# Layer 0 of a graph network: the node's term added in PSUM, the positive parts on ACT, the sums on DVE

## The chip, the cores and the metric

One core of one Trainium2 chip runs one launch of the whole network. The metric is the device time of that launch in microseconds. Engines: PE is TensorE (PEld its weight loads), DVE is VectorE, ACT is ScalarE, POOL is GpSimd, SP is SyncE. The profile is that of one execution; the time before is the median of three runs.

## The reference, cut to what matters

There are 6250 nodes with 64 features and 206250 edges, sorted by their destination. Layer 0 (the only one that the change touches) forms a message for each edge from the features of its destination and 16 features of the edge, and takes the mean of the positive parts at each node:

```python
h = jnp.maximum(_layernorm(x, axis=-1), 0.0)
msg = jax.nn.relu(jnp.concatenate([h[dst], edge_attr_16], -1) @ W1 + b1)
summed = jax.ops.segment_sum(msg, dst, num_segments=N)
aggr = summed / jnp.maximum(count, 1.0)[:, None]
x = x + jax.nn.relu(aggr + h @ Wres + bres)
```

Write A for the node's part of the product (64 rows of `W1`, and `b1`) and E for the edge's part (16 rows of `W1`). A is the same for all edges of a node, so a message is relu(A + E) = max(E, -A) + A. After layer 0 come another normalisation and three attention layers (`L1_gnn`) over the same edges.

## The kernel before, in words

All is in float32. The prologue of `gnn_kernel` ranks the nodes by their degree, so that 49 tiles of 128 nodes are formed in which node p of a tile is row p, and all nodes of a tile have nearly the same number of edges: tile `b` has room for `CAP[b]` edges per node (66, 46, 44, ... 24, 22) and every node of it has at least `LEAST[b]`. `k.full` holds 1 or 0 for each place between the two, whether the node has that edge. `project(q)` (L344) writes for each node a row of `tabx`: with the weights `wn` (L250 to L252) the row holds -A, then A plus the residual product (`Wres`, `bres`), and x from the input.

`layer0` (L480) goes over the tiles `b` in an order written out by hand for POOL, PE, ACT and DVE (`manual_schedule`, L637); each engine takes its instructions in the order in which the code issues them. Per tile: POOL issues the gathers of the edges' features (`load_e`, four tiles ahead, five buffers), of the node rows `rx` (`load_x`), of the sources (`load_src`) and of the attention layers' edge features (`load_ea`), and scatters finished rows (`put`). `turn(b + 1)` transposes the next tile's edge features on PE, eight edges to a 128x128 transpose, and ACT copies them to `eT` (L529). `messages(b, todo)` (L531) then works in blocks of 16 edges: PE multiplies `eT` by the block-diagonal `w0blk` into a `pm` tile (two buffers of two PSUM banks). `r` names the half of the rows of `eT` (0 to 63 or 64 to 127) that hold four edges, and with it the bank; `u` names the group of eight edges. DVE takes max(E, -A) out of PSUM into `msg` (L546 for a full block, L550 and L556 where places may be empty). A tree of additions on DVE sums `msg` (L568). Where at most three places may be empty (`few`), these columns stay out of the tree and are added one by one with their 1 or 0 (L572); in the two tiles with more, they are multiplied by it first (L562).

Between blocks `messages` takes one piece of work of the group of tiles before (`between`): groups of 8, 8, 8, 8, 8, 4, 3 and 2 tiles (`FIN0`) are finished together. `finish(g)` (L575) divides the sums, adds `rx[..., D:2 * D]`, and for a node without edges (it can only be in the last tile) adds back -A (L587 to L592); the positive part plus x is the new x. DVE then takes its mean (L596, L597), and the pieces are: `squares` on ACT (L602), nothing, `norm` on DVE (L606, L608), and per four tiles `project` (transposes on PE into `pt`, ACT into `ht`) and `rows` (products into `po`, L620, ACT to `k.rows`, L622). When all tiles are done a value is read by all engines, and `attention` runs three times: there every edge's row is fetched by one row gather of POOL (`pick`, L466) into `kv`, with products of the edge features (L809) and DVE work on them; the last layer puts rows in place by products with one-hot matrices (L940).

Of the kernel before, what the change touches and what calls it, by code (L numbers as in the profile page):

```python
# [22 lines left out]
F32 = mybir.dt.float32  # L23
# [4 lines left out]
AF = mybir.ActivationFunctionType  # L28
OP = mybir.AluOpType
# [3 lines left out]
P = 128  # L33
N, E, D = 6250, 206250, 64
# [63 lines left out]
def gnn_kernel(ctx: ExitStack, tc: tile.TileContext, x, src_t, dst_t, dst_row, ea16, ea32, eaT16, eaT32, w, out):  # L98
    nc = tc.nc
# [16 lines left out]
    with tc.manual_schedule(engines={getattr(mybir.EngineType, e) for e in ("Pool", "PE", "Activation", "DVE", "SP")}), \  # L116
# [129 lines left out]
        for l in range(LAYERS):  # L246
            nc.gpsimd.memset(k.wblk[l], 0.0)
            for j in range(4):
                nc.sync.dma_start(k.wblk[l][j * 32:(j + 1) * 32, j * D:(j + 1) * D], w[f"L1_gnn_We{l}"])
        wn = p.tile([D + 1, 2 * D], F32, name="wn")  # L250
        nc.gpsimd.tensor_scalar(wn[:, :D], w0[:, :D], -1.0, 0.0, op0=OP.mult, op1=OP.add)
        nc.gpsimd.tensor_add(wn[:, D:], w0[:, :D], w0[:, D:])  # L252
        sff = p.tile([P, T], F32, name="sff")
        nc.gpsimd.tensor_copy(sff, sf)
        for t, values in ((k.cap, CAP), (least, LEAST)):
# [88 lines left out]
        def project(q):  # L344
            po = psum.tile([P, 4, 2 * D], F32, name="pr_o")
            n = len(quads[q])
            for i in range(n):
                nc.tensor.matmul(po[:, i, :], k.ht[q % 2][:, i * P:(i + 1) * P], wn, start=True, stop=True)
# [131 lines left out]
def layer0(tc, ea16, ea32, ident, tabx, srcs, k, col, least, ones, bad, nbad_i):  # L480

    nc = tc.nc
    with tc.tile_pool(name="g0", bufs=3) as gp, tc.tile_pool(name="e0", bufs=2) as ep, \
# [45 lines left out]
                nc.scalar.copy(eT[:, i0:i1], ps[:, :i1 - i0])  # L529

        def messages(b, between):  # L531
            g, c = group[b], CAP[b]
            nega = st["rx", g][:, b - first[g], :D]
            eT = st.pop(("eT", b))
            msg = ep.tile([P, MAXC, D], F32, name="msg")
            for t0 in range(0, c, 16):
                n = min(16, c - t0)
                pm = pp.tile([P, 2, 2, 4, D], F32, name="pm")
                for u in range(2):
                    for r in range(2):  # L540
                        if u * 8 + r * 4 < n:
                            h = slice(r * D, (r + 1) * D)
                            nc.tensor.matmul(pm[:, r, u].rearrange("p j f -> p (j f)"), eT[h, t0 // 8 + u, :],  # L543
                                             k.w0blk[h, :], start=True, stop=True)
                if t0 + 16 <= LEAST[b]:
                    nc.vector.tensor_tensor(msg[:, t0:t0 + 16], pm.rearrange("p r u j f -> p (r u j) f"),  # L546
                                            nega[:, None, :].to_broadcast([P, 16, D]), op=OP.max)
                elif n == 16:
                    for r in range(2):
                        nc.vector.tensor_tensor(  # L550
                            msg[:, t0:t0 + 16].rearrange("p (u r j) f -> p r u j f", u=2, r=2)[:, r], pm[:, r],
                            nega[:, None, None, :].to_broadcast([P, 2, 4, D]), op=OP.max)
                else:
                    for q in range(-(-n // 4)):
                        m = min(4, n - q * 4)
                        nc.vector.tensor_tensor(msg[:, t0 + q * 4:t0 + q * 4 + m], pm[:, q % 2, q // 2, :m],  # L556
                                                nega[:, None, :].to_broadcast([P, m, D]), op=OP.max)
                if between:
                    between.pop(0)()
            few = range(LEAST[b], c) if c - LEAST[b] <= 3 else ()  # L560
            if c > LEAST[b] and not few:
                nc.vector.tensor_mul(msg[:, LEAST[b]:c], msg[:, LEAST[b]:c],  # L562
                                     k.full[:, WOFF[b]:WOFF[b + 1], None].to_broadcast([P, c - LEAST[b], D]))
            total = st["sum", g][:, b - first[g]:b - first[g] + 1, :]
            c -= len(few)
            while c > 1:
                h = c // 2
                nc.vector.tensor_add(msg[:, :h] if c > 2 else total, msg[:, :h], msg[:, c - h:c])  # L568
                c -= h
            for i, j in enumerate(few):  # L570
                w = WOFF[b] + i
                nc.vector.scalar_tensor_tensor(total, msg[:, j:j + 1], k.full[:, w:w + 1], total,  # L572
                                               op0=OP.mult, op1=OP.add)

        def finish(g):  # L575

            n, b0 = FIN0[g], first[g]
            bs = slice(b0, b0 + n)
            rx, s = st.pop(("rx", g)), st.pop(("sum", g))
            wide = lambda t: t[:, :n, None].to_broadcast([P, n, D])  # L580
            c = wp.tile([P, GN], F32, name="cnt")
            nc.vector.tensor_scalar(c[:, :n], k.deg[:, bs], 1.0, None, op0=OP.max)
            nc.vector.reciprocal(c[:, :n], c[:, :n])
            h = wp.tile([P, GN, D], F32, name="h0", bufs=1)
            nc.vector.tensor_mul(h[:, :n], s[:, :n], wide(c))
            nc.vector.tensor_add(h[:, :n], h[:, :n], rx[:, :n, D:2 * D])
            for b in range(b0, b0 + n):  # L587
                if LEAST[b] == 0:
                    alone = wp.tile([P, 1], F32, name="alone")
                    nc.vector.tensor_single_scalar(alone, k.deg[:, b:b + 1], 0.0, op=OP.is_equal)  # L590
                    nc.vector.scalar_tensor_tensor(h[:, b - b0], rx[:, b - b0, :D], alone[:, 0:1], h[:, b - b0],
                                                   op0=OP.mult, op1=OP.add)  # L592
            x = k.x1[:, bs]
            nc.vector.scalar_tensor_tensor(x, h[:, :n], 0.0, rx[:, :n, 2 * D:], op0=OP.max, op1=OP.add)
            m = wp.tile([P, GN], F32, name="m0")
            nc.vector.tensor_reduce(m[:, :n], x, axis=AX.X, op=OP.add)  # L596
            nc.vector.tensor_scalar(m[:, :n], m[:, :n], -1.0 / D, None, op0=OP.mult)  # L597
            v = wp.tile([P, GN], F32, name="v0")
            def squares():
                for i in range(n):  # L600
                    sq = wp.tile([P, D], F32, name="sq")
                    nc.scalar.activation(sq, x[:, i], AF.Square, bias=m[:, i:i + 1], accum_out=v[:, i:i + 1])  # L602
                nc.scalar.activation(v[:, :n], v[:, :n], AF.Sqrt, bias=eps[:, 0:1], scale=1.0 / D)

            def norm():
                nc.vector.reciprocal(v[:, :n], v[:, :n])  # L606
                for i in range(n):
                    nc.vector.tensor_scalar(h[:, i], x[:, i], m[:, i:i + 1], v[:, i:i + 1], op0=OP.add, op1=OP.mult)  # L608

            def project(i0, i1):  # L610
                pt = mp.tile([D, 4 * P], F32, name="pt")
                for i in range(i0, i1):
                    nc.tensor.transpose(pt[:, (i - i0) * P:(i - i0 + 1) * P], h[:, i, :], ident)
                ht = k.ht[i0 // 4 % 2]
                nc.scalar.activation(ht[:D, :(i1 - i0) * P], pt[:, :(i1 - i0) * P], AF.Relu)

            def rows(i0, i, i1):
                po = mp.tile([P, 2, 4 * D], F32, name="po")
                for j in range(i1 - i):
                    nc.tensor.matmul(po[:, j, :], k.ht[i0 // 4 % 2][:, (i - i0 + j) * P:(i - i0 + j + 1) * P], k.ws[0],  # L620
                                     start=True, stop=True)
                nc.scalar.copy(k.rows[:, b0 + i:b0 + i1, :4 * D], po[:, :i1 - i])  # L622

            todo = [squares, lambda: None, norm]
            for i0 in range(0, n, 4):
                i1 = min(n, i0 + 4)
# [9 lines left out]
        wait, todo = [], []  # L636
        with tc.manual_schedule(engines={getattr(mybir.EngineType, e) for e in ("Pool", "PE", "Activation", "DVE")}):  # L637
            for b in range(AHEAD):
                load_e(b)
# [28 lines left out]
            for b in range(NB):  # L668
# [866 lines left out]
```

## Time and profile before

| what | number |
|---|---|
| time, median of 3 runs | 6536.39 us (6527.34 to 6536.92) |
| profiled execution's own time | 6532.44 us |
| its span | 6530.7 us |
| busy PE / PEld | 1956.0 / 1204.2 us |
| busy DVE | 3769.0 us |
| busy ACT | 366.2 us |
| busy POOL | 4828.3 us |
| mean granted TensorE clock | 0.607 |

The span is from the first to the last instruction; busy times are of engines that work side by side and so sum to more than it. The granted clock is a share of TensorE's full clock. In the views a line such as L546 is a line of the kernel before; "xN" counts instructions. A group's row reads: line, engine, operation, what it writes and reads, shape, count, then busy time in us and mean ns of one, then the idle time of the engine just before them and what ended it. A row of waits reads: who waited for whom, us in total, times, the longest.

### The profile page before, as it was taken

The page shows a single profiled execution, that of the slowest core. Times are in us where ns is not written, and L with a number is a line of the kernel's source. Part 1 is how long each engine was busy: PE and PEld are TensorE (multiplying, and loading weights), DVE is VectorE, ACT ScalarE, POOL GpSimd, SP SyncE. Part 2 cuts the span into 40 slices and gives each one's busy share as a digit, 9 for nine tenths or more (in the row PEclk, how much of TensorE's full clock was granted, in tenths as well). Part 3 has the DMA queues.
Part 4 walks back from the last instruction along what each step waited for, and adds up shares of the span by engine and source line. Part 5 has one row for each costly group of instructions (what it writes and reads, how often), then busy time and mean ns, then how long its engine had stood idle before and what let it go on. Part 6 is the DMA issues. An engine that isn't in the chain of part 4 may idle for free. (4 is left out here: it accounts for less than half of the span.)

```text
span 6530.7 us, 28765 instructions
## 1 busy us (share of the span) xinstructions
PE 1956.0 (30%) x5430; PEld 1204.2 (18%) x5430; DVE 3769.0 (58%) x6686; ACT 366.2 (6%) x1266; POOL 4828.3 (74%) x5159
## 2 busy tenths in 40 slices
PE   5762222222222221221222221222333333333342
PEld 3441111111111111111111111111111211121121
DVE  5984545455555553644455545454766666676775
ACT  3220000000000000000000000000000000000000
POOL 4677777777777776777777777776777777777776
PEclk9775555555555555555555555555666666666665
DMA  3674333333333332222222222222222222222222
GB/s 108 221 234 110 81 88 79 85 85 85 83 81 84 83 81 65 72 70 66 69 68 66 69 69 67 70 69 60 71 65 69 65 67 67 67 66 69 65 67 66
DMA packets 242745, 534.93 MB, mean 82 GB/s; under 512 B 101234, under 2 KB 123218, under 8 KB 241458
## 3 DMA queue, kind: packets, MB, share of 16 engines
q0 software_dynamic: 169792, 372.65, 22.7%
q1 hardware_dynamic: 72764, 160.36, 7.8%
q14 instruction: 143, 1.17, 0.1%
q8 instruction: 46, 0.75, 0.0%
HBM read 460.23 MB, written 74.03 MB: 82 GB/s over the span
## 5 line engine op out<-in xcount | busy, mean ns | idle before, releaser
L466 POOL DMA_INDIRECT kv<-tab,src x4788 | 4518.1, 944 | 1499.9 <-issue 1405.9
L820 DVE TENSOR_TENSOR kv<-kv,pe 128x1024 f32<-128x1024 f32 (+7 forms) x666 | 740.1, 1111 | 2237.1 <-DMA kv<-tab,src 2009.4
L809 PE MATMUL pe<-wblk,ea 128*128 128x256 f32 x1740 | 690.6, 553 | 668.4 <-DVE kv L820 598.5
L940 PE MATMUL pos<-only,is_q 128*128 128x448 f32 x616 | 422.6, 799 | 1092.8 <-DVE only L937 1066.8
L914 PE MATMUL pt<-ident,hn 128*64 128x128 f32 x98 | 41.2, 420 | 2131.7 <-DVE hn L909 2110.8
L809 PEld LDWEIGHTS pe<-wblk,ea 128*128 128x128 f32 x1740 | 492.8, 290 | 926.5 <-DVE kv L820 565.3
L866 DVE TENSOR_REDUCE some<-kv 128x64 f32<-128x512 f32 (+3 forms) x693 | 645.4, 931 | 23.9
L809 PE MATMUL pe<-wblk,eaT 128*128 128x256 f32 x870 | 344.7, 561 | 370.7 <-DVE kv L820 347.0
L827 DVE TENSOR_REDUCE al<-prod 128x16 f32<-128x512 f32 (+7 forms) x693 | 438.7, 633 | 24.1
L826 DVE TENSOR_TENSOR prod<-kv,more 128x512 f32<-128x512 f32 (+3 forms) x693 | 438.4, 633 | 24.0
L862 DVE TENSOR_TENSOR kv<-kv,more 128x512 f32<-128x512 f32 (+3 forms) x693 | 431.0, 622 | 0.0
L914 PEld LDWEIGHTS pt<-ident,hn 128*64 128x64 f32 x98 | 12.6, 128 | 2195.4 <-DVE hn L909 2173.8
L940 PEld LDWEIGHTS pos<-only,is_q 128*128 128x128 f32 x616 | 131.6, 252 | 1281.0 <-issue 1087.7
L809 PEld LDWEIGHTS pe<-wblk,eaT 128*128 128x128 f32 x870 | 246.8, 293 | 452.3 <-DVE kv L820 364.7
L947 DVE TENSOR_TENSOR all<-all,pos 128x448 f32<-128x448 f32 x301 | 186.0, 618 | 143.8 <-PE pos L940 135.7
L849 ACT ACTIVATE more<-al,m 128x37 f32<-128x37 f32 (+18 forms) x250 | 73.0, 292 | 2916.1 <-DVE m L844 2891.7
L543 PE MATMUL pm<-w0blk,eT 64*128 64x256 f32 x868 | 171.0, 514 | 91.8 <-DVE msg L546 77.5
L937 DVE TENSOR_TENSOR only<-is_r,more 128x448 f32<-128x448 f32 x308 | 185.1, 613 | 1.5
L466 POOL DMA_INDIRECT e<-in_ea_dram,at_i x98 | 104.9, 1070 | 102.6 <-PE ps L398 39.9
L568 DVE TENSOR_TENSOR msg<-msg 128x128 f32<-128x128 f32 (+12 forms) x221 | 136.2, 616 | 7.1
L543 PEld LDWEIGHTS pm<-w0blk,eT 64*128 64x128 f32 x868 | 110.1, 249 | 136.4 <-DVE msg L546 72.7
L918 PE MATMUL po<-ws,ht 65*128 65x256 f32 x196 | 118.4, 706 | 34.3 <-ACT ht L916 34.3
(217 smaller groups left out, 1737.9 us busy)
## 6 DMA issues: line engine op xcount, KB each, us to landing
kv<-tab,src POOLq DMA_INDIRECT x4788
ea<-eat SPq DMA_DIRECT2D x26, 576.0 KB, 3.8
ea<-eat SPq DMA_DIRECT2D x24, 512.0 KB, 3.4
ea<-eat SPq DMA_DIRECT2D x16, 640.0 KB, 4.0
ean<-e SPq DMA_DIRECT2D x13, 576.0 KB, 3.7
ea<-ean SPq DMA_DIRECT2D x13, 576.0 KB, 4.4
eat<-eaT SPq DMA_DIRECT2D x13, 576.0 KB, 5.6
ea<-eat SPq DMA_DIRECT2D x16, 448.0 KB, 3.4
```

The source lines that it names most:

```text
L466: return nc.gpsimd.indirect_dma_start(out=out, out_offset=None, in_=table, in_offset=bass.IndirectOffsetOnAxis(ap=idx, axis=0))
L543: nc.tensor.matmul(pm[:, r, u].rearrange("p j f -> p (j f)"), eT[h, t0 // 8 + u, :], k.w0blk[h, :], start=True, stop=True)
L568: nc.vector.tensor_add(msg[:, :h] if c > 2 else total, msg[:, :h], msg[:, c - h:c])
L809: nc.tensor.matmul(pe[:, 4 * (g - g0):4 * (g - g0) + 4].rearrange("p j f -> p (j f)"), ea[:, g, :], k.wblk[l], start=True, stop=True)
L820: nc.vector.tensor_add(pair(kv[:, :m, :2 * D]), pair(kv[:, :m, :2 * D]), pe[:, :m, None, :].to_broadcast([P, m, 2, D]))
L826: nc.vector.tensor_mul(prod[:, :n], kv[:, :n, :D], q[:, None, :].to_broadcast([P, n, D]))
L827: nc.vector.tensor_reduce(als[b][:, :H, t0:t0 + n].rearrange("p h j -> p j h"), prod[:, :n].rearrange("p j (h c) -> p j h c", h=H), axis=A ...
L862: nc.vector.tensor_mul(v.rearrange("p j (h c) -> p j h c", h=H), v.rearrange("p j (h c) -> p j h c", h=H), ex[:, :H, t0:t0 + n].rearrange( ...
L866: nc.vector.tensor_reduce(some[:, i, :], v.rearrange("p j f -> p f j"), axis=AX.X, op=OP.add)
L937: nc.vector.tensor_mul(only, is_r[:, rs, None].to_broadcast([P, SG, D]), res[:, None, :].to_broadcast([P, SG, D]))
L940: nc.tensor.matmul(pos[i].rearrange("p r f -> p (r f)"), is_q, only.rearrange("p r f -> p (r f)"), start=True, stop=True)
L947: nc.vector.tensor_add(all_[:, rs], all_[:, rs], pos.pop(i - 1))
```

## The change

A itself is added in PSUM: for each half `r` of a block, PE first multiplies `ident` by A, repeated for each of the half's edges (up to 8, so 512 columns), and then adds the products of the edges on top of it. The loop over `r` is now the outer one, that over `u` the inner. ACT takes the positive part of `pm` into `msg`, with full blocks in one instruction and the rest by groups of four edges; a column of `few` has an instruction of its own, with the 1 or 0 of `k.full` as its scale. So these columns go into the tree of sums, which stands in a new function `add_up`, called right after `messages`. DVE no longer reads PSUM here. The rows of `tabx` are made with `w0` in place of `wn` and hold A and the residual product; the step for nodes without edges goes.

```diff
-        wn = p.tile([D + 1, 2 * D], F32, name="wn")
-        nc.gpsimd.tensor_scalar(wn[:, :D], w0[:, :D], -1.0, 0.0, op0=OP.mult, op1=OP.add)
-        nc.gpsimd.tensor_add(wn[:, D:], w0[:, :D], w0[:, D:])
...
-                nc.tensor.matmul(po[:, i, :], k.ht[q % 2][:, i * P:(i + 1) * P], wn, start=True, stop=True)
+                nc.tensor.matmul(po[:, i, :], k.ht[q % 2][:, i * P:(i + 1) * P], w0, start=True, stop=True)
...
-            nega = st["rx", g][:, b - first[g], :D]
+            a = st["rx", g][:, b - first[g], :D]
             eT = st.pop(("eT", b))
             msg = ep.tile([P, MAXC, D], F32, name="msg")
+            few = range(LEAST[b], c) if c - LEAST[b] <= 3 else range(0)
             for t0 in range(0, c, 16):
                 n = min(16, c - t0)
                 pm = pp.tile([P, 2, 2, 4, D], F32, name="pm")
-                for u in range(2):
-                    for r in range(2):
-                        if u * 8 + r * 4 < n:
-                            h = slice(r * D, (r + 1) * D)
-                            nc.tensor.matmul(pm[:, r, u].rearrange("p j f -> p (j f)"), eT[h, t0 // 8 + u, :],
-                                             k.w0blk[h, :], start=True, stop=True)
+                for r in range(2):
+                    us = [u for u in range(2) if u * 8 + r * 4 < n]
+                    if us:
+                        nc.tensor.matmul(pm[:, r, :len(us)].rearrange("p u j f -> p (u j f)"), ident,
+                                         a[:, None, :].to_broadcast([P, 4 * len(us), D]), start=True, stop=False)
+                    h = slice(r * D, (r + 1) * D)
+                    for u in us:
+                        nc.tensor.matmul(pm[:, r, u].rearrange("p j f -> p (j f)"), eT[h, t0 // 8 + u, :],
+                                         k.w0blk[h, :], start=False, stop=(u == us[-1]))
                 if t0 + 16 <= LEAST[b]:
-                    nc.vector.tensor_tensor(msg[:, t0:t0 + 16], pm.rearrange("p r u j f -> p (r u j) f"),
-                                            nega[:, None, :].to_broadcast([P, 16, D]), op=OP.max)
...
+                    nc.scalar.activation(msg[:, t0:t0 + 16], pm.rearrange("p r u j f -> p (r u) j f"), AF.Relu)
                 else:
                     for q in range(-(-n // 4)):
                         m = min(4, n - q * 4)
-                        nc.vector.tensor_tensor(msg[:, t0 + q * 4:t0 + q * 4 + m], pm[:, q % 2, q // 2, :m],
-                                                nega[:, None, :].to_broadcast([P, m, D]), op=OP.max)
+                        t = t0 + q * 4
+                        f = len([i for i in few if t <= i < t + m])
+                        if m > f:
+                            nc.scalar.activation(msg[:, t:t + m - f], pm[:, q % 2, q // 2, :m - f], AF.Relu)
+                        for i in range(m - f, m):
+                            w = WOFF[b] + t + i - LEAST[b]
+                            nc.scalar.activation(msg[:, t + i], pm[:, q % 2, q // 2, i], AF.Relu, scale=k.full[:, w:w + 1])
                 if between:
                     between.pop(0)()
-            few = range(LEAST[b], c) if c - LEAST[b] <= 3 else ()
+            sums.append((b, msg, few))
+
+        def add_up():
+
+            b, msg, few = sums.pop(0)
+            g, c = group[b], CAP[b]
             if c > LEAST[b] and not few:
...
             total = st["sum", g][:, b - first[g]:b - first[g] + 1, :]
-            c -= len(few)
             while c > 1:
                 h = c // 2
                 nc.vector.tensor_add(msg[:, :h] if c > 2 else total, msg[:, :h], msg[:, c - h:c])
                 c -= h
-            for i, j in enumerate(few):
-                w = WOFF[b] + i
-                nc.vector.scalar_tensor_tensor(total, msg[:, j:j + 1], k.full[:, w:w + 1], total,
-                                               op0=OP.mult, op1=OP.add)
...
-            for b in range(b0, b0 + n):
-                if LEAST[b] == 0:
-                    alone = wp.tile([P, 1], F32, name="alone")
-                    nc.vector.tensor_single_scalar(alone, k.deg[:, b:b + 1], 0.0, op=OP.is_equal)
-                    nc.vector.scalar_tensor_tensor(h[:, b - b0], rx[:, b - b0, :D], alone[:, 0:1], h[:, b - b0],
-                                                   op0=OP.mult, op1=OP.add)
...
                 messages(b, todo)
+                add_up()
```

In the kernel after, the identity product is its line L541, the edges' product L545, the positive parts L548, L555 and L558, the tree L573.

More of the change, by code (lines that the diff above doesn't have):

```diff
@@ L538, in messages @@
                 pm = pp.tile([P, 2, 2, 4, D], F32, name="pm")
-                for u in range(2):
-                    for r in range(2):
-                        if u * 8 + r * 4 < n:
-                            h = slice(r * D, (r + 1) * D)
-                            nc.tensor.matmul(pm[:, r, u].rearrange("p j f -> p (j f)"), eT[h, t0 // 8 + u, :],
-                                             k.w0blk[h, :], start=True, stop=True)
-                if t0 + 16 <= LEAST[b]:
-                    nc.vector.tensor_tensor(msg[:, t0:t0 + 16], pm.rearrange("p r u j f -> p (r u j) f"),
-                                            nega[:, None, :].to_broadcast([P, 16, D]), op=OP.max)
[L548 to L552, printed above, removed]
+                for r in range(2):
[7 more added lines that the diff above has]
+                                         k.w0blk[h, :], start=False, stop=(u == us[-1]))
+                if t0 + 16 <= LEAST[b]:
+                    nc.scalar.activation(msg[:, t0:t0 + 16], pm.rearrange("p r u j f -> p (r u) j f"), AF.Relu)
                 else:
@@ L635, in layer0 @@
         AHEAD, LATE, LATER = 4, 6, 6
-        wait, todo = [], []
+        wait, todo, sums = [], [], []
         with tc.manual_schedule(engines={getattr(mybir.EngineType, e) for e in ("Pool", "PE", "Activation", "DVE")}):
```

## The prediction

> **What bounds the kernel now.** First the page, to see which stage has which limit. Its rows by slice, and the costliest group:
>
> ```profile
> DVE  5984545455555553644455545454766666676775
> POOL 4677777777777776777777777776777777777776
> PEclk9775555555555555555555555555666666666665
> L466 POOL DMA_INDIRECT kv<-tab,src x4788 | 4518.1, 944 | 1499.9 <-issue 1405.9
> ```
>
> A slice is 163 us. From the fourth slice on POOL issues row gathers: 4788 of 944 ns, each followed by some 0.3 us "issue", together 6018 us. That is the attention part, and the change does not touch it. The second question is how long layer 0 lasts, so I cut the span where layer 0's first product starts, where its last one ends, and where the first gather of the attention part is issued:
>
> ```profile
> 127.00:468.00 341.00, 242.16 (x1219) 162.88 (x1217) 317.27 (x604) 73.38 (x251) 240.97 (x227) 0.77 0.67 213
> 468.00:499.50 31.50, 7.88 (x20) 3.99 (x17) 12.40 (x42) 4.02 (x16) 18.17 (x17) 0.50 0.75 233
> 499.50:6530.00 6030.50, 1641.64 (x3954) 991.35 (x3954) 3382.78 (x5901) 231.84 (x824) 4523.06 (x4793) 0.59 0.28 73
> ```
>
> Columns: stretch, length, busy PE, PEld, DVE, ACT, POOL (instructions), granted clock, DMA share, GB/s. In the 341 us that the change touches DVE is busy 317 us (93%), PE 242, POOL 241, ACT 73. The groups by line and the waits say the same from the other side:
>
> ```profile
> L543 PE MATMUL pm<-w0blk,eT 64*128 64x256 f32 x868 | 171.0, 514 | 91.8 <-DVE msg L546 77.5 <-ACT sq L602 13.9 <-DMA e<-in_ea_dram,at_i 0.2
> L546 DVE TENSOR_TENSOR msg<-pm,rx 128x1024 f32<-128x1024 f32 x76 | 90.4, 1217 | 2.0 <-PE pm L543 1.9
> L556 DVE TENSOR_TENSOR msg<-pm,rx 128x256 f32<-128x256 f32 (+3 forms) x110 | 35.3, 369 | 7.7 <-PE pm L543 7.5
> POOL e L466 <- PE turn L528: 33.5, 13, 6.5
> ```
>
> PE waits 77.5 us for DVE to free `pm`; DVE waits 9.4 us for PE in these rows, and POOL waits for PE (33.5 us, for the buffer of `e`). So DVE bounds layer 0. What decides the forecast is how far away PE is, and that its timeline tells:
>
> ```profile
> 250.86 2.00 PE L543 MATMUL pm<-w0blk,eT 64*128 64x256 f32 x16
> 258.02 3.79 PE L543 MATMUL pm<-w0blk,eT 64*128 64x256 f32 x16
> 4664.15 1.03 PE L809 MATMUL pe<-wblk,ea 128*128 128x256 f32 x4
> 103.08 1.06 PE L340 MATMUL pr_t<-ident,hn 128*64 128x128 f32 x4
> 103.93 1.91 PE L348 MATMUL pr_o<-wn,ht 65*128 65x128 f32 x8
> ```
>
> Columns: start, us, then the records merged. One f32 matmul leaves two records, a transpose one. At full clock four records of 256 columns with 128 rows take 1.03 us (0.216 each plus the drain); 16 records of the same columns with 64 rows take 2.00, half as much each. The products of the two halves (`r` = 0 on rows 0 to 63, `r` = 1 on rows 64 to 127), issued in turn, run side by side. The second row is the same work at half clock.
>
> **The change, part by part.** *DVE loses*: 76 x L546 (90.4 us), 10 x L550 at 682 ns (6.4), 110 x L556 (35.3), 47 x L572 (13.4), two instructions of the lone-node fix (0.4): 146 us. The tree of sums takes 47 more columns of 64: 3 us by the 1.04 ns per element between its 128x512 (692) and 128x1024 (1222) rows. DVE falls from 317 to about 174 us.
>
> *ACT gains* 76 positive parts of 128x1024 from PSUM. No row shows that width; ACT's 128x128 takes 272 ns and 128x512 takes 585 (L529), so 0.815 per column and 1.00 us: 76 us. 81 quads of 128x256 at 378: 31. 37 shorter ones at 220 to 325: 10. 47 single columns with a scale: between 220 (the slope) and 335 (L602, with a bias operand); I take 300: 14. Sum 131, ACT 73 + 131 = 204 us: not a bound.
>
> *PE gains* 194 identity products of 512 columns and 46 of 256, and loses the side-by-side run, because `u` is now the inner loop: an identity product on all rows, two products on the same 64 rows, then the same for the other half. Where two neighbouring products lie on different halves, an identity product on all rows stands between them, so nothing runs beside anything. At full clock (0.2133 per 256 columns and record): identity 194 x 2 x 0.427 + 46 x 2 x 0.2133 = 185 us; products 434 x 2 x 0.2133 = 185; 230 transposes L528 and 49 L613 at 0.107 = 30; 49 row products L620 = 21. Sum 421 us, where the old order at full clock had 93 + 51 = 144. A block of 16 edges costs PE 3.41 us instead of 0.85. 421 exceeds 341: PE becomes the bound, if nothing is smaller than these rows say.
>
> [...] The L809 row (all rows, new weights each record) goes at 0.216 per record with its weight loads of about 0.19 hidden, so the sum goes without.
>
> *The clock.* 421 is for full clock; the stage's granted clock is 0.77 now. Rows 103.08 and 103.93 belong to 17 us in which PE is never idle and yet streams 128 columns in 0.213, half pace (the page has no clock record there). So density is not enough. I took every window of 3.413 us of the trace in which the clock stood at half, and worked out the share (columns streamed x rows/128) of what the array could take: above 0.75 the next window was at full clock, below not, in all but 2 of 1504. From full it fell below about 0.4. The new stream, half identity (1.0) and half 64-row products (0.5), is at exactly 0.75 at half clock, above only where transposes stand. So: once at full it stays; a wait of over about 2 us drops it; it is up again at the next tile's transposes.
>
> [...]
>
> *Waits that are left.* ACT now stands between PE and DVE. Behind a group's `squares` (ACT waits for DVE's mean: tree 3.4 + chain L582 to L597 3.5, then 8 x 0.34 + 0.3) queue the next positive parts, and PE waits for the second `pm` buffer: ACT is free at about 11 us after the old tile's last block, PE needs the buffer at about 9 (three blocks and the transposes) in tiles of over 32 edges. With 7 group ends at 0.3 to 3 us and `pt`/`po` waits of 1 us (now 8.6 on DVE h and 3.1 on ACT rows in all): 20 us, bounds 5 and 45. Each drop costs between half a window (1.7) and a tile at half pace (8.6): 7 drops, 28 us, bounds 0 and 60.
>
> *Nothing else moves.* `wn` costs POOL two instructions of 0.55 us in the prologue, before PE waits for ACT's L335 anyway. POOL's 227 instructions keep their order, 241 us busy in a longer stage; the transfers stay 0.67 of 341 us. The tail of 31.5 us runs from the last product through rows, scatter and `ean`, in the same order. The gathers of 6018 us start later and take as long.
>
> Sum: stage 420 (the first tile's transposes lie ahead) + 20 + 28 = 468 instead of 341: +127. The profiled execution took 6532.4 (span 6530.7), 4 below the median of the runs: 6536 + 127 = 6663 us.
>
> **Rivals.** *PE bound at half clock.* The knife edge at 0.75 goes the other way and transposes do not lift the clock, or every wait drops it for long. Then the stage is between 600 and 842 + 10 us: 6800 to 7045, say 6900. For it: the 17 us above. Against: first blocks in the old trace rise at once behind transposes (granted 1.00 from 129 us on).
>
> *Faster: the identity product is cheap.* If it streams in one pass, as a transpose against the same `ident` does (one record, 0.107 per 128 columns), PE sums to 421 - 92 = 329. Then PE and its waits race with the old 341: it is faster if the waits stay under 12 us, at best by 12 (6524). Against: L809, L940 and L348 all leave two records for a plain f32 matmul, and the identity product is a plain one.
>
> *No difference.* PE's added work hidden: the stage would need 421 us of streaming in 341, which asks for side-by-side runs that the order excludes.
>
> **How the numbers follow.** Forecast 0.86, its own range 6622 to 6722 (a stage of 421 + 5 + 0 to 421 + 45 + 60, so +86 to +186); half clock 0.08; cheap identity 0.04, half of it faster; no difference 0.02. The range for 8 in 10 is that one: it leaves out the rivals (0.14) and next to nothing of the forecast. This kernel's runs can tell about 0.2% (13 us) from no change. Faster 0.02, same 0.04, slower 0.94.
>
> **What would show it.** Right: DVE near 174 us in the stage and ACT near 204; PE over 85% busy and waited for by ACT positive parts and DVE; an L541 group of 480 records with 0.43 us between two of 512 columns; no waits of PE on DVE `msg`; a stage of 450 to 490 us at a granted clock over 0.9; attention unchanged at 6030 us. Wrong: granted clock under 0.75 (first rival), 240 records on L541 (second), or PE waiting on ACT for more than 60 us.

## The result, and the profile after

| | kernel before | kernel after |
|---|---|---|
| median | 6536.66 us (6527.34 to 6542.28, 4 runs) | 6717.88 us (6712.29 to 6728.74, 4 runs) |
| ratio to before | 1 | 1.0279, interval 1.0265 to 1.0293 |
| span of the profiled execution | 6530.7 us | 6721.2 us |

The change costs 181 us where 127 were forecast; the time lies inside the range (6622 to 6722), near its upper end. The page of the kernel after, its rows by slice and two groups:

```profile
PE   6999222222222222121222222222233333333442
DVE  4334454555555555444455445455576666667775
PEclk8999555555555555555555555555566666666665
L573 DVE TENSOR_TENSOR msg<-msg 128x960 f32<-128x960 f32 (+19 forms) x224 | 140.1, 625 | 300.1 <-ACT msg L558 241.1
```

Slices 2 to 4 now read 9 on PE and 3, 3, 4 on DVE, where DVE read 9 and 8 in slices 2 and 3 before: the bound has moved to PE. The same cut by stages as before (first product to last product, then the tail to the first gather of the attention part; the stage is cut once more where the clock rises):

```profile
122.60:160.30 37.70, 37.70 (x64) 16.17 (x62) 7.11 (x4) 6.47 (x15) 13.51 (x13) 0.50 0.21 60
160.30:656.00 495.70, 494.06 (x1638) 247.79 (x1638) 180.15 (x371) 182.62 (x476) 235.65 (x222) 1.00 0.47 151
656.00:680.00 24.00, 5.84 (x17) 3.09 (x14) 7.74 (x25) 4.29 (x18) 8.20 (x9) 0.56 0.37 119
680.00:6721.20 6041.20, 1659.94 (x3954) 1002.49 (x3954) 3380.99 (x5901) 232.08 (x824) 4532.63 (x4793) 0.59 0.25 73
```

The stage lasts 533 us, 192 more than before, and in it PE (second number) is busy all but 1.6 us. DVE has 187 us in the two stretches, ACT 189. The clock is 0.50 for the first 38 us and 1.00 for the remaining 496. The tail is 7.5 us shorter, and the attention part 10.7 longer in this execution; in the second profiled execution of the same kernel (f1 below) it is 6030.9, so that is no part of the change. The groups of PE's two kinds of product:

```profile
L545 PE MATMUL pm<-w0blk,eT 64*128 64x256 f32 x868 | 258.9, 415 | 0.0
L541 PE MATMUL pm<-rx,ident 128*128 128x512 f32 (+1 forms) x480 | 253.0, 610 | 1.0 <-ACT msg L548 1.0
```

480 records of the identity, two for each of 240 products; and idle time of 1.0 us ahead of them: PE waits for nobody. Who waits now is the rest:

```profile
DVE msg L573 <- ACT msg L558: 241.1, 36, 10.0
POOL e L463 <- PE turn L525: 190.9, 40, 20.8
```

With 421 us of streaming and no waits the stage should take 421 us plus what half clock costs. PE's timeline says where the rest is. Start, length, records; first two rows at half clock, then at full clock:

```profile
126.67 2.08 PE L541 MATMUL pm<-rx,ident 128*128 128x512 f32 x2
128.68 2.07 PE L545 MATMUL pm<-w0blk,eT 64*128 64x256 f32 x4
...
306.12 0.77 PE L525 MATMUL turn<-ident,e 128*128 128x128 f32 x5
306.73 1.02 PE L541 MATMUL pm<-rx,ident 128*128 128x512 f32 x2
307.68 1.13 PE L545 MATMUL pm<-w0blk,eT 64*128 64x256 f32 x4
308.74 1.12 PE L541 MATMUL pm<-rx,ident 128*128 128x512 f32 x2
309.79 1.13 PE L545 MATMUL pm<-w0blk,eT 64*128 64x256 f32 x4
310.85 1.12 PE L541 MATMUL pm<-rx,ident 128*128 128x512 f32 x2
```

From 308.74 to 310.85 one half of a block (two identity records, four product records) takes 2.11 us; streaming it takes 2 x 0.427 + 4 x 0.213 = 1.71. The 0.40 us lie at the two changes between records of 128 rows and of 64. Single records, start to start: product to identity 0.305 instead of 0.213, first to second identity record 0.530 instead of 0.427, identity to product 0.520, first to second product record 0.320, the others at their pace. The weight loads show the same; PEld's timeline of the same stretch:

```profile
308.74 0.30 PEld L541 LDWEIGHTS pm<-rx,ident 128*128 128x128 f32 x2 [0.33 <-issue]
309.79 0.73 PEld L545 LDWEIGHTS pm<-w0blk,eT 64*128 64x128 f32 x4 [0.76 <-issue]
310.85 0.30 PEld L541 LDWEIGHTS pm<-rx,ident 128*128 128x128 f32 x2 [0.33 <-issue]
```

The first load of each new kind starts together with its own record (308.74, 309.79, 310.85) and not during the record before: it is uncovered. 240 halves x 0.40 = 97 us. The sum is then 421 + 97 + 17 for the start at half clock (38 us of half pace, of which some 17 would not be there at full) = 535, measured 533. Between transposes (128 rows) and an identity product (128 rows) there is no such gap: 0.110 from start to start. Nor does every other change of the row count cost something; the row products (L615) have 65 rows:

```profile
268.05 0.70 PE L545 MATMUL pm<-w0blk,eT 64*128 64x256 f32 x2
268.67 1.13 PE L615 MATMUL po<-ws,ht 65*128 65x256 f32 x4
269.64 0.71 PE L525 MATMUL turn<-ident,e 128*128 128x128 f32 x5
```

From 64 to 65 rows the first record starts after 0.306 us and the second after 0.320, as from 64 to 128. From 65 to 128 rows all 21 neighbours at full clock start 0.216 us apart, at their pace. So in this trace the loss stands between a record of 64 rows and one of more rows, and below "change of row count" means that.

### The profile page after: what moved, and what is told of

It reads as the page before. It is cut to its first block, busy times and chain, and to the rows that moved or that the text cites. A ratio compares the mean times of both kernels' runs of the same rounds, so it can differ in the third digit from the quotient of the medians.

```text
span 6721.2 us, 29740 instructions
## 1 busy us (share of the span) xinstructions
PE 2256.4 (34%) x5910; PEld 1309.7 (19%) x5910; DVE 3633.2 (54%) x6444; ACT 481.6 (7%) x1507; POOL 4835.8 (72%) x5157
## 5 line engine op out<-in xcount | busy, mean ns | idle before, releaser
L573 DVE TENSOR_TENSOR msg<-msg 128x960 f32<-128x960 f32 (+19 forms) x224 | 140.1, 625 | 300.1 <-ACT msg L558 241.1
L545 PE MATMUL pm<-w0blk,eT 64*128 64x256 f32 x868 | 258.9, 415 | 0.0
L541 PE MATMUL pm<-rx,ident 128*128 128x512 f32 (+1 forms) x480 | 253.0, 610 | 1.0 <-ACT msg L548 1.0
L545 PEld LDWEIGHTS pm<-w0blk,eT 64*128 64x128 f32 x868 | 147.4, 191 | 181.7 <-issue 169.4
```

The costliest lines, as they stand in the source:

```text
L541: nc.tensor.matmul(pm[:, r, :len(us)].rearrange("p u j f -> p (u j f)"), ident, a[:, None, :].to_broadcast([P, 4 * len(us), D]), start=Tru ...
```

## The experiments

My theory after the result: what was missing in the sum is a loss of 0.2 us at each change of row count on PE. Rivals: a product that accumulates into the bank just written waits for the product before it; and the path from PE by ACT to DVE is itself longer than the old one from PE to DVE. The first four kernels ran on a chip on which the kernel before takes 7774 us (15 runs), the others on chips on which it takes 6528, so times are compared only within one chip.

**e1: no identity product.** The old order of products, and ACT's part as in the change.

```diff
-                        nc.tensor.matmul(pm[:, r, :len(us)].rearrange("p u j f -> p (u j f)"), ident,
-                                         a[:, None, :].to_broadcast([P, 4 * len(us), D]), start=True, stop=False)
...
+                for u in range(2):
+                    for r in range(2):
+                        if u * 8 + r * 4 < n:
...
+                                             k.w0blk[h, :], start=True, stop=True)
```

> The changed kernel without the identity products: A is left out of the messages, and the edges' products come in the old order (u outer, r inner). ACT takes the positive parts and DVE the sums as in the changed kernel. Theory (all of the loss is PE's identity products and the lost pairing): PE's stream falls to 144 us at full clock, DVE stays at 180 us and ACT at 187 us in the stage, and POOL's 227 instructions with 0.3 us of issue each, some 310 us, are what is left: stage 300 to 320 us, time 6500 to 6525. Rival (the longer path PE, ACT, DVE costs by itself): the stage stays at 341 us or more, time 6536 or more.

Measured: 7749.40 us, ratio 0.9968 (0.9953 to 0.9983), 25 us faster than before on this chip. The stage is 368 us where 300 to 320 were expected (h1 below repeats it on a 6528 us chip). DVE is busy 182 us from 127 to 490, ACT 181, PE 233. So the move of the positive parts to ACT costs nothing, it gains; the whole loss goes with the identity products on PE. The rival about the path falls.

**e2: no identity product, the loop over r outside.** As e1, with the two loops changed over as the change has them.

```diff
-                for u in range(2):
-                    for r in range(2):
+                for r in range(2):
+                    for u in range(2):
                         if u * 8 + r * 4 < n:
```

> As the run without identity products (A is left out), but with r as the outer loop, so that two products on the same 64 rows follow each other and none run side by side. PE's stream is 236 us at full clock and 472 at half. If the clock goes by the share of the array's rows in use, a dense stream of 64-row products is at 0.5, under the 0.75 that lifts it and over the 0.4 that drops it: it is lifted only around transposes, the granted clock of the stage is 0.6 to 0.8, and the stage 340 to 400 us (6536 to 6600). If it goes by PE being busy, the granted clock is over 0.9 and the stage as without identity products in the old order, 300 to 320 us (6500 to 6525).

Measured: 7758.92 us, ratio 0.9979 (0.9965 to 0.9994). A row of PE's timeline:

```profile
253.61 1.14 PE L542 MATMUL pm<-w0blk,eT 64*128 64x256 f32 x8
```

Eight records of a block in 1.14 us, as when issued in turn: the products of the upper and the lower half run side by side although four records of one half are issued before the first of the other. So the order of the loops by itself loses nothing; the identity product on all rows between the halves does. What e2 should have said about the clock it can't say, since its stream was not the unpaired one.

**e3: both identity products first, then the products in turn.**

```diff
+                us = [[u for u in range(2) if u * 8 + r * 4 < n] for r in range(2)]
                 for r in range(2):
...
+                    if us[r]:
+                        nc.tensor.matmul(pm[:, r, :len(us[r])].rearrange("p u j f -> p (u j f)"), ident,
+                                         a[:, None, :].to_broadcast([P, 4 * len(us[r]), D]), start=True, stop=False)
+                for u in range(2):
+                    for r in range(2):
+                        if u in us[r]:
...
+                                             k.w0blk[h, :], start=False, stop=(u == us[r][-1]))
```

> The changed kernel with both identity products of a block first and then the edges' products with u outer and r inner, as before the change. Same instructions, another order. Theory (each change between 128-row and 64-row records leaves two weight loads uncovered, about 0.4 us per run of products): 421 - 92 us of streaming for the pairs, and 127 blocks x 0.41 = 52 us instead of 240 halves x 0.41 = 97; the share of rows in use is 1.0, so that the clock is up from the first window: stage 385 us, time 6580 (6565 to 6595). Rival (a product that adds to what another has just put into its bank waits for it): the excess of 97 us stays, stage 430, time 6620.

Measured: 7824.76 us, ratio 1.0055 (1.0034 to 1.0077), +51 us. It was run again beside the change's own time on a 6528 us chip (g3 below), where the reading stands.

**e4: products on all 128 rows.** `w0blk` gets a column block for each of the eight edges, so that a group of eight is one product of 512 columns; identity and products then all have 128 rows and nothing runs side by side. It streams as much as the change: 421 us. To make room, two small tiles (`sq`, and `ns` behind layer 0) have fewer buffers.

```diff
-            nc.sync.dma_start(k.w0blk[j * 16:(j + 1) * 16, j % 4 * D:(j % 4 + 1) * D], w["L0_gnn_W1"][D:, :])
+            nc.sync.dma_start(k.w0blk[j * 16:(j + 1) * 16, j * D:(j + 1) * D], w["L0_gnn_W1"][D:, :])
...
+                for u in range(-(-n // 8)):
+                    m = 4 * min(2, -(-(n - 8 * u) // 4))
+                    nc.tensor.matmul(pm[:, u].rearrange("p r j f -> p (r j f)")[:, :m * D], ident,
+                                     a[:, None, :].to_broadcast([P, m, D]), start=True, stop=False)
+                    nc.tensor.matmul(pm[:, u].rearrange("p r j f -> p (r j f)")[:, :m * D], eT[:, t0 // 8 + u, :],
+                                     k.w0blk[:, :m * D], start=False, stop=True)
```

> The changed kernel with the edges' products on all 128 rows: the block-diagonal weights are 512 columns wide, and one product does eight edges (217 products of up to 512 columns instead of 434 of 256 columns), so that identity products and edges' products have the same rows. The streamed columns of PE are the same 421 us. Theory (uncovered weight loads at changes of the number of rows): none are left, each record goes at its streaming pace of 0.427 us per 512 columns, the clock is up from the first window, stage 425 to 435 us, time 6620 (6605 to 6635). Rival (adding on top of the identity product in the same bank waits): the excess of 97 us stays, stage 520, time 6705.

Measured: 7839.86 us, ratio 1.0075 (1.0054 to 1.0095), +66 us. At full clock the records of 512 columns start 0.43 us apart: two take 0.86 us, from 299.53 to 300.39 and from there to 301.25 in its timeline.

**f1, f2: the change and the kernel before once more, and f4: e4 once more, on one chip.**

> The changed kernel itself, beside the others of this group. 181 us slower than before on the chip of the first measurement. The runs without identity products and the two other orders came from a chip on which the kernel before takes 7774 us; if this group runs on one like it, the same 181 us are expected (PE's stream does not depend on what made the rest slower), some 20 to 40 less if the waits that this chip adds lie on DVE in the old order and are covered by PE here.

> The kernel before, for its trace on the same chip as the others of this group: the stage of the messages from the first to the last product, 341 us in the first trace. If a chip's slowness sits in layer 0 too, the stage is near 390 us (the runs without identity products had 368 us there and were 25 us faster than before).

> The products on 128 rows once more, now beside the changed kernel itself. Uncovered weight loads (240 halves x 0.41 = 97 us) and the 33 us at half clock at the stage's start (16 us) are what sets the two apart, so 113 us faster than the changed kernel, 70 slower than before.

Measured: f1 6709.27 us, ratio 1.0272 (1.0256 to 1.0288), +181; f2 has one run, 6529.1, with a stage of 339 us; f4 6632.39, ratio 1.0158 (1.0143 to 1.0174), +104. With the same streaming, the same ACT and the same DVE work, products on all rows save 77 us of the change's 181; 113 were expected. f4's timeline of PE:

```profile
299.39 1.02 PE L540 MATMUL pm<-rx,ident 128*128 128x512 f32 x2
300.25 1.02 PE L542 MATMUL pm<-w0blk,eT 128*128 128x512 f32 x2
301.11 1.02 PE L540 MATMUL pm<-rx,ident 128*128 128x512 f32 x2
```

and of its weight loads:

```profile
299.40 0.19 PEld L540 LDWEIGHTS pm<-rx,ident 128*128 128x128 f32 x1 [0.24 <-issue]
299.82 0.19 PEld L542 LDWEIGHTS pm<-w0blk,eT 128*128 128x128 f32 x1 [0.24 <-issue]
300.25 0.19 PEld L542 LDWEIGHTS pm<-w0blk,eT 128*128 128x128 f32 x1 [0.24 <-issue]
```

Two records each 0.86 us, 0.43 apiece, new weights or not, and the load for the product that starts at 300.25 stands at 299.82, one record ahead. Each product here accumulates into the bank that the identity has just written, as in the change, and does not wait: that rival falls too. By windows of one stretch, f1 first and then f4 (the granted clock of f1's row, 1.00, says nothing of the time before 190.7 us, where the records of the clock begin):

```profile
127.00:560.00 433.00, 432.03 (x1326) 212.29 (x1325) 143.44 (x274) 143.28 (x353) 190.74 (x178) 1.00 0.44 135
```

```profile
127.00:560.00 433.00, 417.58 (x1226) 212.92 (x1225) 179.31 (x354) 181.77 (x463) 243.12 (x229) 0.97 0.55 172
```

That f1 ran at half pace until then, its timeline shows:

```profile
185.27 2.07 PE L545 MATMUL pm<-w0blk,eT 64*128 64x256 f32 x4
...
192.66 1.13 PE L545 MATMUL pm<-w0blk,eT 64*128 64x256 f32 x4
```

f4 has nearly finished (stage 449 us) when f1 has done four fifths (stage 545): in the same time DVE did 179 us of its work in one and 143 in the other. Now that PE is nearer to the others it also waits, 15 us. The stages differ by 96 us; by the theory 97 for the changes and about 31 for f1's start at half clock (until 190.7 us), less f4's waits of 15 and its own half clock of about 12: 101. The expectation had left f4's waits and half clock out. The medians differ by less than the stages, because f1's profiled execution (6729.4) was the slowest of its four.

**g3: e3 on a 6528 us chip.**

> e3_identity_then_pairs once more, on whatever chip this call gets. Where the kernel before takes about 6530 us, its stage of 446 us on the other chip should shrink like the kernel before's did there: TensorE has 185 of identity + about 100 of paired products + 30 of transposes + 21 of row products = 336 us, plus waits of 20-45: stage 360-390 us, time +20 to +50 us, ratio 1.003-1.008; the version of the change, unpaired, had 1.027. Rival: the pairing is not what the change lost, and the stage is again over 440 us, ratio above 1.015.

Measured: 6591.83 us, ratio 1.0096 (1.0080 to 1.0112), +64; stage 411. The direction is that of the theory, the size is not (360 to 390). PE's timeline:

```profile
303.66 1.88 PE L541 MATMUL pm<-rx,ident 128*128 128x512 f32 x4
305.48 1.13 PE L547 MATMUL pm<-w0blk,eT 64*128 64x256 f32 x8
```

A block takes 2.88 us instead of the change's 4.22: one change in each direction instead of two, and the products side by side. I had left the changes of row count out of the expectation: 127 blocks x 0.40 = 51 us, which makes 336 + 51 = 387, plus 15 us of waits = 402. The granted clock of the stage, 0.97 over 411 us, is worth up to 14 us more, which covers the last 9.

**f3: shared out between the engines.** 62 of the 76 full blocks stay on DVE as max(E, -A) without an identity product (n·A added once per tile as a column of the tree); the rest goes as in e3 by PE and ACT.

```diff
+                on_dve = t0 + 16 <= LEAST[b] and (t0 == 0 or b % 2 == 0)
+                if not on_dve:
...
+                if on_dve:
+                    nc.vector.scalar_tensor_tensor(msg[:, t0:t0 + 16], a[:, None, :].to_broadcast([P, 16, D]), -1.0,
+                                                   pm.rearrange("p r u j f -> p (r u) j f"), op0=OP.mult, op1=OP.max)
+                    more += 16
...
+            if more:
+                nc.scalar.activation(msg[:, c], a, AF.Copy, scale=float(more))
```

> Both ways side by side. 62 of the 76 full blocks go by max(E, -A) on DVE (one scalar_tensor_tensor that takes A times -1), without an identity product; 14 full and all partial blocks go by identity products (both first, then the products) and positive parts on ACT, which also puts 16 or 32 times A as one more column into the tree; the sums of a tile come after the first block of the next tile. Theory (what costs is PE's stream, what is gained is DVE's time): PE 185 - 62 x 1.71 = 79 us of identity, 93 of paired products, 51 of the rest and some 45 of uncovered loads, 268 us; DVE 180 + 62 x 1.13 + 5 = 255 us; POOL's issue, some 310 us, is the longest: 15 to 25 us faster than before. Rival (ACT between PE and DVE costs waits by itself): as before or slower.

Measured: 6531.23 us, ratio 1.0005 (0.9996 to 1.0014): no difference, where 15 to 25 us of gain were expected. Its windows and waits:

```profile
127.00:460.00 333.00, 285.33 (x1433) 167.77 (x1432) 258.51 (x435) 132.54 (x471) 242.21 (x220) 0.94 0.67 214
```

```profile
DVE msg L553 <- PE pm L550: 57.5, 31, 8.1
PE pm L544 <- DVE msg L553: 34.3, 18, 6.7
```

PE is busy 285 us and DVE 259, each under the 311 that DVE has in f2's same stretch, but they wait for each other, and the stage stays at 337 us.

**g1: all 76 full blocks on DVE.**

```diff
-                on_dve = t0 + 16 <= LEAST[b] and (t0 == 0 or b % 2 == 0)
+                on_dve = t0 + 16 <= LEAST[b]
```

> f3_shared_out with all 76 full blocks of 16 kept off the identity (maximum with -A on VectorE, n·A added once per tile); only the partly filled blocks take A on TensorE and their positive parts on ScalarE. Against f3 the identity records of 14 more full blocks go: 14 x 4 x 0.43 = 24 us less of TensorE (285 to about 261), and 14 x about 1.05 = 15 us more of VectorE (258 to about 273). If the two engines waited for each other because blocks of the two kinds alternate, the stage shrinks from 337 to 320-330 us and the ratio is 0.997-0.999. Rival: the 48 us of TensorE's idle time come from VectorE being behind, in which case 15 us more on VectorE keep the stage at 335-345 us and the ratio at 1.000.

Measured: 6523.68 us, ratio 0.9992 (0.9983 to 1.0001). The stage is 332 us, between the 320 to 330 of the theory and the 335 to 345 of the rival; the gain of 4 us can't be told from none.

**g2: the identity product in 16-bit parts.** As e3, with A split into two bf16 parts (and `sq` in one buffer, to make room).

```diff
+        def split(b):
+            a = st["rx", group[b]][:, b - first[group[b]], :D]
+            h = st["a", b] = wp.tile([P, 2, D], BF16, name="a_h", bufs=2)
+            nc.scalar.copy(h[:, 0], a)
+            nc.vector.tensor_sub(h[:, 1], a, h[:, 0])
...
+                        for i in range(2):
+                            nc.tensor.matmul(pm[:, r, :len(us[r])].rearrange("p u j f -> p (u j f)"), ident_h,
+                                             a[:, i:i + 1, :].to_broadcast([P, 4 * len(us[r]), D]), start=(i == 0), stop=False)
```

> e3_identity_then_pairs with A split into two parts of 16-bit type (a rounded part and the rest, 40 copies on ScalarE, 40 subtractions on VectorE), both added by a 16-bit identity; what is left of A beyond the two parts is left out. [...] The stage of e3 was bounded by TensorE; with 92 us less there it comes to ScalarE (187 + 40 x 0.2 = 195 us of work) and VectorE (184) and waits between them: stage 300-330 us against 340 before, ratio 0.994-0.999. Rival: that each of the four products of a half waits for the sum in its bank to be written, or the loads of the weights show, as with the 64-row records: then 0.2 us per half more, and the stage stays at 340-380, ratio 1.000-1.006.

Measured: 6527.84 us, ratio 1.0000 (0.9991 to 1.0009). A row of 512 columns leaves one record, 0.22 from start to start, so an identity product in two parts streams 0.43 us where g3's streams 0.85. The 92 us less on PE that the expectation takes had been shown by no run when it was put down; by these records it is right, and of it the time keeps 64 us against g3. The stage is 333 us, although no engine but PE (300 of 333 us) is over three quarters busy. The expected 300 to 330 were missed.

**h1: e1 on a 6528 us chip.** The kernel before, f3, g1 and g2 share out the work quite differently and all have a stage of 332 to 340 us. Something else stands close behind.

> e1_no_identity once more (A left out of every message; VectorE 182, ScalarE 181, TensorE 233 us of work in the stage). Four kernels with quite different loads (the kernel before, f3, g1, g2) all have a stage of 332 to 340 us. Theory: GpSimd's queue is right behind: 245 gathers and scatters of this stage start 1.25 us apart (0.94 busy and 0.30 in which it waits for nothing), 306 us, and what it waits for e buffers comes on top; then this kernel, with no engine but GpSimd over 70% busy, still has a stage of 315-332 us and GpSimd is busy or between two of its own instructions for over 290 of the 323 us from 127 to 450; ratio 0.996-0.999. Rival: the stage of 332-340 comes from the handovers between TensorE, ScalarE and VectorE; with all three at 0.55-0.7 the stage falls to 270-300 us, ratio 0.990-0.994.

Measured: 6506.99 us, ratio 0.9969 (0.9957 to 0.9981); the stage is 305 us, 34 less than in f2 (another chip, on which the kernel before takes the same 6528 us), of which the time keeps 21: the tail up to the first gather of the attention part is 41 us long here and 28 in f2. The windows of f2, g2 and h1 over one stretch (the last of the five busy times is POOL):

```profile
127.00:450.00 323.00, 225.61 (x1165) 152.34 (x1164) 303.39 (x569) 69.07 (x236) 231.94 (x215) 0.80 0.67 215
```

```profile
127.00:450.00 323.00, 291.77 (x1648) 162.58 (x1646) 187.25 (x407) 192.40 (x512) 231.37 (x216) 0.93 0.67 215
```

```profile
127.00:450.00 323.00, 232.00 (x1234) 153.20 (x1233) 193.80 (x399) 191.67 (x508) 254.18 (x230) 0.80 0.71 229
```

and POOL's waits of h1 in it, and its timeline:

```profile
POOL e L463 <- issue: 20.6, 68, 0.3
POOL src L463 <- issue: 14.0, 46, 0.3
POOL rx L463 <- issue: 12.2, 40, 0.3
POOL tab L469 <- issue: 11.0, 36, 0.3
POOL e L463 <- PE turn L525: 0.9, 3, 0.3
```

```profile
298.23 0.94 POOL L463 DMA_INDIRECT src<-srcs,at_i  x1 [0.30 <-issue]
299.47 0.94 POOL L463 DMA_INDIRECT e<-in_ea_dram,at_i  x1 [0.30 <-issue]
300.72 0.94 POOL L463 DMA_INDIRECT e<-in_ea_dram,at_i  x1 [0.31 <-issue]
301.97 0.95 POOL L463 DMA_INDIRECT rx<-tabx,num_i  x1 [0.30 <-issue]
```

POOL starts its shortest gathers every 1.25 us, and waits for PE's transposes 0.9 us in all, where it waits 28.5 in f2 and 26.8 in g2. In the whole stage of h1, 217 of its instructions start, nearly all gathers and scatters; they are busy 238 us, and between no two of them lie more than 0.32 us (65 us in all). So in h1 POOL is the bound, with no other engine over three quarters busy. The theory's sum, 245 at 1.25 = 306, meets the 305 by luck: some of the 245 lie in the tail, and many take longer than the shortest, so that the mean from start to start is 1.40 us. In the stages of f2, f3, g1 and g2 POOL's work with 0.3 us between two instructions comes to some 305 to 315 us as well, and the rest, 19 to 27 us, is waiting, mostly for PE's transposes. I had expected 315 to 332; the theory's bound is right and the waits I put on top are nearly absent.

## Why the prediction was right, by its steps

**The bound moves from DVE to PE: right.** DVE fell to 187 us in the stage (174 forecast), ACT rose to 189 (204), and PE went from 242 to 532 of 533. e1 shows that without the identity product the same ACT and DVE work is faster than before.

**The streaming of 421 us: right, but the reason given for the lost pairing was half wrong.** There are 480 identity records, those of 512 columns 0.43 us from start to start where nothing is lost, as forecast, and no cheap pass. The prediction blamed also the inner loop over `u`; e2 has it and keeps the halves side by side. The identity product on all rows is what parts them: four records of products take 1.13 us between two of them in the profile after, eight take 1.14 in e2.

**The weight loads at nothing: the step that failed.** The prediction took them as hidden, from the L809 row. That row is of records of 128 rows behind records of 128 rows, and for such neighbours it holds: in f4's rows each load stands one record ahead (299.82 for the record at 300.25), and the records are 0.43 us apart without a gap. Where 64 rows follow 128 or the reverse, the first load starts only with its own record (308.74 and 309.79 in the profile after): 0.2 us a change, two changes for each half, 97 us. In the trace of before such neighbours stand only where products meet transposes or row products, at the ends of tiles and between blocks, and the prediction did not measure those: at full clock 0.306 us pass there from the last product's record to the first of the next kind, where 0.216 is the pace. The miss of the stage, 65 us (533 for 468), is, to 3 us, this 97 less the 29 that waits and clock fell short. Two of the prediction's own signs failed with it: the stage of 450 to 490 us, and the 0.43 us between the two records of an identity product, which are 0.53 wherever a product of 64 rows stands before. That the time still lies in the range is luck: its upper end allowed 45 us for waits and 60 for half clock, which came to 2 and 17, and a term that had no place in the sum filled that room.

**The waits of 20 us: too many.** PE waits under 2 us in the stage. The prediction had ACT come free some 2 us too late at a group's end; but a block takes PE 4.2 us instead of the 3.4 that it reckoned with, so the positive parts are always done. In f4, where a block takes 3.4 us, the waits are 15 us: the estimate was right for the stream that it was made for.

**The half clock of 28 us: near in size by luck, for another cause.** There are no drops at waits, for there are no waits. All of it lies at the start: with the uncovered loads a half takes 4.01 us at half clock and fills 0.64 of the array's rows by columns (1.71 us on all rows and 1.71 on half of them), below the 0.75 that the prediction read off the windows of the trace before, and tile 0's eight halves run at half pace until transposes come (157.0 us; full clock from 160.3): 17 us lost, and 31 in f1, where tile 1 stayed slow as well. A busy PE was not enough: it ran 38 us in the first profile and 64 us in f1 at half pace without a pause of 0.1 us. Once up, the clock does not fall in the stage (1.00 over 495.7 us). f4, whose products all have 128 rows, has a granted clock of 0.97 over its 449 us.

**The rest: right.** POOL's order and the attention part have not moved (6030.9 and 6031.4 us in f1 and f2); the tail became 7.5 us shorter, which was not forecast: POOL had more time to work off its queue. The rivals at half clock throughout and with a cheap identity did not occur.

The sum with the measured terms is 421 + 97 + 17 = 535 instead of 420 + 20 + 28 = 468; the stage measured 533 us.

## What to carry to other kernels

On PE, count the changes between records of 64 rows and records of more, and not only the columns: here each costs 0.2 us (from 65 rows to 128 nothing is lost, 0.216 us from start to start), and one matmul kind laid out on the same rows as its neighbours (f4, +104 us) or grouped with its own kind (g3, +64) was cheaper than the same columns interleaved (f1, +181). Moving a cheap DVE operand onto PE pays only if PE has the time: here it bought DVE 130 us and cost PE 290. And before balancing engines, look at the one that paces the stage from behind: at 1.40 us a gather or scatter on average POOL left 35 us of a stage of 340 to be won, whatever was done on the other three.

## What the runs showed that I had not expected

- In e2 products on different halves of the rows ran side by side though they were not issued in turn: eight records in 1.14 us, with four of one half issued first.
- In f4 a weight load of 0.19 us was covered by a record of the same 128 rows (start to start 0.43 us for 512 columns). In the profile after it was not where 64 rows follow more or the reverse (0.09 us lost before the first record and 0.105 us before the second at each change); from 65 rows to 128 nothing was lost (21 neighbours, 0.216 us apart).
- In f4 a product that accumulates into the PSUM bank that the product before it wrote did not wait for it: it starts 0.86 us after the identity product, which is that product's two records of 0.43.
- In g2 a bf16 product of 512 columns left one record of 0.22 us, where the f32 one left two of 0.43 in f4.
- The kernel before takes 7774 us on one chip and 6528 on others; the ratio of e3 is 1.0055 on the first and 1.0096 on the other, so a ratio from one chip does not carry over.
